# The first MLP of a four-layer transformer block kernel: second layer by token, contexts loaded earlier, norm and modulation on another engine

## The chip, the cores and the metric

The kernel runs on one core of a Trainium2 chip. Five engines work side by side, each through its own instructions in the order in which they were issued, and wait for each other by semaphores: TensorE (PE in the profile, with its weight loads as PEld), VectorE (DVE), ScalarE (ACT), GpSimd (POOL) and SyncE (SP), whose queue issues the DMA transfers of this kernel. The metric is the device time of one execution in microseconds (us). Before the change it is 1635.87 us, the median of three runs (1634.98 to 1640.96).

## The reference

The input `x` has 128 batches of 64 tokens with 128 features; `cond` has one vector of 128 for each batch, `ctx` 64 tokens for each batch. Four layers follow one another, all in float32. What the change touches is the last third of the first layer:

```python
mod = silu(t_emb) @ adaln_w + adaln_b
sh_sa, sc_sa, g_sa, sh_ff, sc_ff, g_ff = split(mod[:, None, :], 6)
...
xm = _ln(x) * (1.0 + sc_ff) + sh_ff
h = gelu(xm @ fc1_w + fc1_b, approximate=True)
x_ff = h @ fc2_w + fc2_b
x = x + g_ff * x_ff
```

`_ln` is a layer norm without weights, `fc1_w` is 128 x 512, `fc2_w` 512 x 128. Ahead of this the layer has a self attention and a cross attention; layer 1 is a cross attention with modulated norms of its own, layer 2 has the form of layer 0 with normed contexts, layer 3 is a mixture of experts.

## The kernel before

The 8192 tokens lie in 16 groups of 512 (8 batches); a group is a tile `xs[s]` of 128 partitions x 4 x 128, where a partition is a token and the last axis the features. All 16 groups stay in SBUF for the whole kernel. The order of all instructions is written out by hand: each engine takes them as the Python code emits them.

The stages are: the attentions of layer 0 (self, then cross, 16 groups each, `steps_1`), the first MLP (`turns_0`), the three attentions of layers 1 and 2 (`steps_2`), the second MLP (`turns_2`), layer 3. The last seven attention steps overlap the start of the following MLP, and the last turns of an MLP hold the preparation of the next stage: `into_mlp` (L1199) puts five heads of the MLP between attention steps, then turns 0 to 3 beside the last four steps, which close the last groups (`finish`, L522, with its normalization L548, bias L550 and projection L554). From turn 11 on `ahead_2` prepares the first groups of layer 1 (`prepare`, L378).

One MLP turn j (L733) works on several groups at once: the norm of group j+2, the hidden layer of group j in four parts, the output layer of group j-1 in four parts between them, the entry (transposition and modulation) of group j+1, the statistics of group j+3. In the first MLP the steps are as follows.

- `measure` (L662): layer norm statistics by VectorE (L312, L314), 1/std by GpSimd (L321, and a power, L322).
- `norm` (L665): GpSimd negates the mean (L361) and norms the four quarters (L364).
- `enter` (L668): four transposes on TensorE (L334, `psT`), then `modulated` (L337): VectorE multiplies (L339), GpSimd adds (L340), and the result `xm` has the features in the partitions.
- `hidden` (L671): a matmul of 128 x 512 (L675) and a gelu on ScalarE (L676).
- `output` (L678): the result `py` has features in the partitions; four parts accumulate (L681).
- `gate` (L704): VectorE adds the bias and multiplies by the gate (L706).
- `leave` (L711), one turn later: four transposes turn the result back to tokens (L714, `psB`), VectorE adds it to `xs` (L715) and takes the statistics that layer 1 will need (`x_mv`).
- `measure_context` (L646), in `beside_0` (L1180): SP loads the context of group j (L649), VectorE takes its statistics, GpSimd makes two reciprocal deviations and two products (L653, L321, L322, L656). They are used by layers 1 and 2. Beside it the tables for later layers are made (`later_tables`, L284), one piece in each of the first turns.

The second MLP has the forms `output_by_token` (L686, four matmuls of 128 x 128 for each quarter of the tokens, L691), `bias_by_token` (L696, L697 on GpSimd) and `leave_by_token` (L699; L701 and L702 on VectorE), which need no transposition: tokens are in the partitions of `py` at once. The gate and the gate times the bias then must lie in token layout; they come from a small table in DRAM (`gate_table`, L214), from which `gate_tile` (L273) loads 256 KB for each group by two broadcasting DMAs (L278).

`modulated_by_batch` (L343) is used by the attentions: ScalarE does the multiplication and the addition at once, one instruction for each of the 8 batches of a group (L351). SBUF tiles of one tag take turns in two buffers as a rule ("cm" for the contexts, "gt" for the gates), and so do the PSUM tiles "mm" (psT, psB, tables); "ph" has four buffers, "py" two.

Of the kernel before, what the change touches and what calls it, by code (L numbers as in the profile page):

```python
# [9 lines left out]
F32 = mybir.dt.float32  # L10
AF = mybir.ActivationFunctionType
ALU = mybir.AluOpType
# [3 lines left out]
P = 128  # L16
NST = 16
TT = 4
NB = 8
L = 64  # L20
NT = TT * P
# [38 lines left out]
def tile_kernel(ctx: ExitStack, tc: tile.TileContext, a: dict, out: bass.AP):  # L60
    nc = tc.nc
    V, S, G, T = nc.vector, nc.scalar, nc.gpsimd, nc.tensor
# [3 lines left out]
    def const(shape, name):  # L66
        return cp.tile(shape, F32, tag=name, name=name)

    x_d = a["x"].rearrange("b n c -> (b n) c").rearrange("(s t p) c -> s p t c", t=TT, p=P)
    ctx_d = a["ctx_1024"].rearrange("b n c -> (b n) c").rearrange("(s t p) c -> s p t c", t=TT, p=P)  # L70
# [11 lines left out]
    w = {}  # L82
# [11 lines left out]
    xs = [const([P, TT, P], f"x{s}") for s in range(NST)]  # L94
# [12 lines left out]
    for name, n in (("L0_xcond_ca_proj_b", P), ("L1_xcond_bp", P), ("L2_xcond_b_cproj", P), ("L3_xcond_router_b", 3)):  # L107
        t = const([P, n], name)
# [10 lines left out]
    ident = const([P, P], "ident")  # L119
# [7 lines left out]
    class Places:  # L127
# [9 lines left out]
    pools = [  # L137
        Places(),
        stack.enter_context(tc.tile_pool(name="mm", bufs=2, space=PSUM)),
        None,  # L140
        None,
        None,
    ]
# [38 lines left out]
    def col(name, i=0):  # L182
        r = _ROW[name] + i
        return vec[:, r : r + 1]
# [83 lines left out]
    def in_two(f, *of):  # L268

        kept = []  # L270
        return lambda: kept.append(f(*of)), lambda: kept[0]()
# [23 lines left out]
    def mod(name, i, s):  # L295

        return mods[name][:, i, ts(s, NB)].unsqueeze(2).broadcast_to([P, NB, L])

    def by_batch(t):
        return t.rearrange("p (b l) -> p b l", b=NB)  # L300
# [6 lines left out]
    x_mv = const([P, NST, TT, 2], "x_mv")  # L307

    def stats(pool, src, mv):
        st = pool.tile([P, TT, 6], F32, tag="st", name="st")  # L310
        for t in range(TT):
            V.bn_stats(st[:, t, :], src[:, t, :])  # L312
        for t in range(TT):
            V.bn_aggr(mv[:, t, :], st[:, t, :])  # L314
# [15 lines left out]
    def transposed(psum, src):  # L330

        ps = psum.tile([P, 512], F32, tag="mm", name="psT")
        for t in range(TT):
            T.transpose(ps[:, ts(t, P)], src[:, t, :], ident)  # L334
        return ps

    def modulated(pool, ps, name, scale, shift, s, tag="xm"):  # L337
        xm = pool.tile([P, NT], F32, tag=tag, name=tag)
        V.tensor_tensor(by_batch(xm), by_batch(ps), mod(name, scale, s), ALU.mult)  # L339
        G.tensor_tensor(by_batch(xm), by_batch(xm), mod(name, shift, s), ALU.add)  # L340
        return xm
# [17 lines left out]
    def normed_by_pool(pool, src, mv, rs, tag, engine=G):  # L359
        nmu = pool.tile([P, TT], F32, tag="nmu" + tag, name="nmu")  # L360
        G.tensor_scalar(nmu, mv[:, :, 0], -1.0, 0.0, ALU.mult, ALU.add)  # L361
        xn = pool.tile([P, TT, P], F32, tag=tag, name=tag)
        for t in range(TT):
            engine.tensor_scalar(  # L364
                xn[:, t, :], src[:, t, :], nmu[:, t : t + 1], rs[:, t : t + 1], ALU.add, ALU.mult
            )
        return xn
# [275 lines left out]

    def measure_context(s):  # L646
        pool = pools[0]
        c = pool.tile([P, TT, P], F32, tag="cm", name="c")
        nc.sync.dma_start(c, ctx_d[s])  # L649
        mv = pool.tile([P, TT, 2], F32, tag="mvc", name="mvc")  # L650
        stats(pool, c, mv)
        nmu = pool.tile([P, TT], F32, tag="nmuc", name="nmuc")
        G.tensor_scalar(nmu, mv[:, :, 0], -1.0, 0.0, ALU.mult, ALU.add)  # L653
        for eps in ctx_rs:
            rs = power(ctx_rs[eps][:, s], mv, eps)
            G.tensor_tensor(ctx_nb[eps][:, s], nmu, rs, ALU.mult)  # L656

    def mlp(wmod, w1, b1, w2, b2, beside, mv_out=None, by_token=False):

        pool, psum = pools[:2]  # L660

        def measure(d):  # L662
            d["mv"], d["rs"] = stats_of(pool, xs[d["s"]], 1e-6)

        def norm(d):  # L665
            d["xn"] = normed_by_pool(pool, xs[d["s"]], d["mv"], d["rs"], "xn")

        def enter(d):  # L668
            d["xm"] = modulated(pool, transposed(psum, d["xn"]), wmod, 4, 3, d["s"])

        def hidden(d, f):  # L671
            if f == 0:
                d["h"] = pool.tile([P, 4, NT], F32, tag="e", name="h")
            ph = pools[2].tile([P, 512], F32, tag="ph", name="ph")
            T.matmul(ph, w[w1][:, 0, ts(f, P)], d["xm"], start=True, stop=True)  # L675
            S.activation(d["h"][:, f, :], ph, AF.Gelu_apprx_tanh, bias=col(b1, f))  # L676

        def output(d, f):  # L678
            if f == 0:
                d["py"] = pools[3].tile([P, 512], F32, tag="py", name="py")  # L680
            T.matmul(d["py"], w[w2][:, f, :], d["h"][:, f, :], start=f == 0, stop=f == 3)  # L681

        def gates_of(d):
            d["gt"] = gate_tile(pool, d["s"], w2)

        def output_by_token(d, t):  # L686

            if t == 0:
                d["py"] = pools[3].tile([P, TT, P], F32, tag="py", name="py")
            for f in range(4):  # L690
                T.matmul(  # L691
                    d["py"][:, t, :], d["h"][:, f, ts(t, P)], w[w2][:, f, :],
                    start=f == 0, stop=f == 3,
                )

        def bias_by_token(d):  # L696
            G.tensor_tensor(xs[d["s"]], xs[d["s"]], d["gt"][:, :, 1, :], ALU.add)  # L697

        def leave_by_token(d):  # L699
            y = pool.tile([P, TT, P], F32, tag="y", name="y")  # L700
            V.tensor_tensor(y, d["py"], d["gt"][:, :, 0, :], ALU.mult)  # L701
            V.tensor_add(xs[d["s"]], xs[d["s"]], y)  # L702

        def gate(d):  # L704
            d["y"] = pool.tile([P, NT], F32, tag="y", name="y")
            V.scalar_tensor_tensor(  # L706
                by_batch(d["y"]), by_batch(d["py"]), col(b2), mod(wmod, 5, d["s"]),
                ALU.add, ALU.mult,
            )

        def leave(d):  # L711
            pt = psum.tile([P, 512], F32, tag="mm", name="psB")
            for t in range(TT):
                T.transpose(pt[:, ts(t, P)], d["y"][:, ts(t, P)], ident)  # L714
            V.tensor_add(xs[d["s"]], xs[d["s"]], pt.rearrange("p (t c) -> p t c", t=TT))  # L715
            if mv_out is not None:
                stats(pool, xs[d["s"]], mv_out[:, d["s"]])

        ds = [dict(s=s) for s in range(NST)]

        def go(f, j, *more):
            if 0 <= j < NST:
                f(ds[j], *more)

        heads = [
            lambda: go(measure, 0),
            lambda: go(norm, 0),
            lambda: go(measure, 1),
            lambda: (go(enter, 0), go(norm, 1)),
            lambda: go(measure, 2),  # L730
        ]

        def turn(j):  # L733
            out = output_by_token if by_token else output
            go(norm, j + 2)
            go(hidden, j, 0)
            go(out, j - 1, 0)
            go(hidden, j, 1)
            go(out, j - 1, 1)
            go(enter, j + 1)  # L740
            go(measure, j + 3)
            if by_token:
                go(bias_by_token, j - 1)
            go(hidden, j, 2)
            go(out, j - 1, 2)
            if 0 <= j < NST:
                beside(j)
            go(hidden, j, 3)
            go(out, j - 1, 3)
            if by_token:  # L750
                go(leave_by_token, j - 1)
                go(gates_of, j)
            else:
                go(gate, j - 1)
                go(leave, j - 2)

        return heads, [lambda j=j: turn(j) for j in range(NST + 2)]


# [412 lines left out]
    def stages():  # L1172
        ats = [attention_of(s, layer) for layer in ("L0s", "L0c") for s in groups]
        ats[0]["first"] = True
        ahead_1, steps_1 = attend(pools, ats)
# [3 lines left out]

        def beside_0(j):  # L1180
            measure_context(j)
            if j < len(later_tables):
                later_tables[j]()

        def beside_2(j):
            for f in l3_parts.get(j - 4, ()):
                f()

        heads_0, turns_0 = mlp(
            "L0_xcond_adaln_w", "L0_xcond_fc1_w", "L0_xcond_fc1_b", "L0_xcond_fc2_w",  # L1190
            "L0_xcond_fc2_b", beside_0, mv_out=x_mv,
        )
        heads_2, turns_2 = mlp(
            "L2_xcond_W_mod", "L2_xcond_W_mlp1", "L2_xcond_b_mlp1", "L2_xcond_W_mlp2",
            "L2_xcond_b_mlp2", beside_2, by_token=True,
        )
        last = 5

# [32 lines left out]
            f()  # L1231
        first_mods[2]()
        n = last + 2 + len(heads_0)
        for f in steps_1[6:-n]:
            f()
        rest = into_mlp(steps_1, heads_0, turns_0)
        second = [(0, 1, 2), (0,), (1, 0), (0, 0, 1, 2), (0, 1, 1, 2, 0, 0, 3, 3)]
        n_ = len(second)
# [66 lines left out]
```

## Time and profile before

| | |
|---|---|
| median of the runs | 1635.87 us |
| the profiled execution | 1636.9 us |
| its span, first to last instruction | 1635.1 us |
| mean granted TensorE clock | 0.994 |
| busy: PE, DVE, ACT, POOL | 97%, 79%, 64%, 66% |
| first hidden matmul of the first MLP to first scores of layer 1 | 412.51 to 552.91 us |

Of the views used below, the stretches give the busy time of each engine between two moments. A timeline row gives the start, the duration, the engine, the line, the operation with the tiles written and read, and how many instructions were merged; a bracket is idle time of the engine ahead of it and what ended it. Names drop their digits: `L_xcond_fc_w` is `fc1_w` or `fc2_w` of layer 0, `L_xcond_W_mlp` those of layer 2. A matmul of float32 takes two instructions, and their ends are modelled, so the distance from one start to the next is the better measure of TensorE.

### The profile page before, as it was taken

The page shows a single profiled execution, that of the slowest core. Times are in us where ns is not written, and L with a number is a line of the kernel's source. Part 1 is how long each engine was busy: PE and PEld are TensorE (multiplying, and loading weights), DVE is VectorE, ACT ScalarE, POOL GpSimd, SP SyncE. Part 2 cuts the span into 40 slices and gives each one's busy share as a digit, 9 for nine tenths or more (in the row PEclk, how much of TensorE's full clock was granted, in tenths as well). Part 3 has the DMA queues.
Part 4 walks back from the last instruction along what each step waited for, and adds up shares of the span by engine and source line. Part 5 has one row for each costly group of instructions (what it writes and reads, how often), then busy time and mean ns, then how long its engine had stood idle before and what let it go on. Part 6 is the DMA issues. An engine that isn't in the chain of part 4 may idle for free.

```text
span 1635.1 us, 64936 instructions
## 1 busy us (share of the span) xinstructions
PE 1581.5 (97%) x27842; PEld 1090.9 (67%) x27842; DVE 1296.4 (79%) x2430; ACT 1038.6 (64%) x1714; POOL 1079.4 (66%) x1814
## 2 busy tenths in 40 slices
PE   6999999998999899999999999998999999999998
PEld 4677767776554467777777677776777666666665
DVE  6999989999566688899999999998454566666666
ACT  5778767776333587788887888886334544444443
POOL 5688777775899888986787786665876333333322
PEclk9999999999999999999999999999999999999999
DMA  7333443322202012211333432221432111111100
GB/s 208 82 93 85 109 118 87 93 81 60 62 27 58 27 47 72 63 47 47 95 86 92 102 99 62 72 56 53 125 91 77 31 37 40 39 34 33 36 11 20
DMA packets 146783, 112.71 MB, mean 69 GB/s; under 512 B 36357, under 2 KB 125247, under 8 KB 146495
## 3 DMA queue, kind: packets, MB, share of 16 engines
q1 hardware_dynamic: 146288, 108.53, 25.0%
q8 instruction: 219, 3.59, 0.9%
q14 instruction: 69, 0.57, 0.1%
q10 hardware_dynamic: 207, 0.03, 0.0%
HBM read 83.99 MB, written 14.02 MB: 60 GB/s over the span
## 4 chain that ended last, share of the span: by engine, by line
PE 79%; DVE 13%; ACT 3%; POOL 2%; issue 1%; DMA 1%; SPq 1%; POOLq 0%; DVEq 0%
PE sc L470 9%; PE pp L495 9%; PE po L512 7%; PE ph L1062 6%; PE ph L675 6%; PE ph L1063 6%; DVE mx L477 5%; DVE e L479 5%; PE po L1093 5%; PE psT L334 5%; PE pk L428 5%; PE py L554 4%; PE py L691 3%; PE pvv L451 3%; PE pq L441 3%; PE py L681 2%
## 5 line engine op out<-in xcount | busy, mean ns | idle before, releaser
L499 ACT ACTIVATE eT<-pp 128x1024 f32<-128x1024 f32 x320 | 329.8, 1030 | 162.5 <-PE pp L495 162.5
L477 DVE TENSOR_REDUCE mx<-sc 128x32 f32<-128x2048 f32 x160 | 366.6, 2291 | 61.8 <-PE sc L470 61.8
L479 DVE TENSOR_TENSOR e<-sc,mx 128x2048 f32<-128x2048 f32 x160 | 366.6, 2291 | 5.4
L495 PEld LDWEIGHTS pp<-ident,e 64*128 64x128 f32 x5120 | 185.1, 139 | 142.6 <-ACT eT L499 46.7
L436 POOL TENSOR_SCALAR kbd<-kT,mask 128x512 f32<-128x512 f32 x316 | 212.4, 689 | 44.0 <-ACT kT L430 41.2
L495 PE MATMUL pp<-ident,e 64*128 64x64 f32 x5120 | 228.9, 229 | 8.4 <-DVE e L479 4.7
L364 POOL TENSOR_SCALAR xn<-x,nmu,rs 128x128 f32<-128x128 f32 x508 | 223.0, 452 | 13.3
L548 POOL TENSOR_TENSOR oT<-o,rb 128x512 f32<-128x512 f32 x80 | 102.0, 1275 | 153.1 <-DMA rb<-recs 65.8
L470 PE MATMUL sc<-kbd,qT 32*64 32x256 f32 x5120 | 181.7, 391 | 16.2 <-DVE e L479 15.3
L676 ACT ACTIVATE h<-ph,vec 128x512 f32<-128x512 f32 x128 | 87.4, 688 | 153.1 <-PE ph L675 152.9
L512 PE MATMUL po<-eT,vbd 128*32 128x64 f32 x10240 | 178.6, 222 | 1.2 <-issue 1.2
L1069 ACT ACTIVATE h<-h 128x512 f32<-128x512 f32 x112 | 70.5, 630 | 148.0 <-DVE h L1065 129.1
L512 PEld LDWEIGHTS po<-eT,vbd 128*32 128x32 f32 x10240 | 152.1, 110 | 14.0 <-issue 1.7
L322 POOL TENSOR_TENSOR rs<-rs,nhalf 128x4 f32<-128x4 f32 x128 | 130.3, 1018 | 10.6
L470 PEld LDWEIGHTS sc<-kbd,qT 32*64 32x64 f32 x5120 | 98.3, 132 | 53.5 <-DVE e L479 19.3
L1065 DVE TENSOR_TENSOR h<-ph,ab 128x512 f32<-128x512 f32 x112 | 77.0, 688 | 55.7 <-PE ph L1063 55.5
L312 DVE BATCH_NORM_STATS2 st<-x 128x6 f32<-128x128 f32 x512 | 110.5, 278 | 0.6
L1098 DVE SCALAR_TENSOR_TENSOR acc<-po,pr,acc 128x128 f32<-128x128 f32 x192 | 67.3, 350 | 44.1 <-PE po L1093 39.5
L1062 PE MATMUL ph<-nx,w 128*128 128x512 f32 x192 | 99.9, 602 | 0.0
L520 ACT COPY o<-po 128x512 f32<-128x512 f32 x160 | 95.7, 598 | 5.7 <-PE po L512 3.5
L1063 PE MATMUL ph<-u,w_ev 128*128 128x512 f32 x192 | 98.0, 592 | 0.0
L1093 PEld LDWEIGHTS po<-w_2o,h 128*128 128x128 f32 x768 | 92.1, 192 | 8.7 <-issue 8.4
(261 smaller groups left out, 2851.8 us busy)
## 6 DMA issues: line engine op xcount, KB each, us to landing
rb<-recs SPq DMA_DIRECT2D x80, 256.0 KB
c<-in_ctx_dram SPq DMA_DIRECT2D x64, 256.0 KB
o<-o SPq DMA_DIRECT2D x320, 32.0 KB
gt<-gate_L_xcond_sa_proj_w SPq DMA_DIRECT2D x32, 256.0 KB
gt<-gate_L_xcond_W_proj SPq DMA_DIRECT2D x32, 256.0 KB
gt<-gate_L_xcond_W_mlp SPq DMA_DIRECT2D x32, 256.0 KB
x<-in_x_dram SPq DMA_DIRECT2D x16, 256.0 KB
ctxT<-cm SPq DMA_DIRECT2D x16, 256.0 KB
```

Source lines behind the costliest of these rows:

```text
L322: G.tensor_tensor(rs, rs, nhalf, ALU.pow)
L364: engine.tensor_scalar(xn[:, t, :], src[:, t, :], nmu[:, t : t + 1], rs[:, t : t + 1], ALU.add, ALU.mult)
L436: (V if at.get("first") else G).tensor_scalar(kbd[:, j], by_batch(kT), mask[:, j : j + 1], 1.0, ALU.mult, ALU.mult)
L470: T.matmul(sc[ts(h, L), g, ts(t2, 256)], qT[ts(g, 32), ts(b, L)], kbd[ts(g, 32), :, b, :], start=True, stop=True,)
L477: V.tensor_reduce(mx, sc.rearrange("p g (m k) -> p (g m) k", k=L), AX.X, ALU.max)
L479: V.tensor_tensor(e, sc.rearrange("p g (m k) -> p (g m) k", k=L), mx.unsqueeze(2).broadcast_to([P, 32, L]), ALU.subtract,)
L495: T.transpose(pp[:, h, ts(4 * g2 + 2 * i + t2, L)], e6[ts(h, L), 2 * gg + g2, t2, i], ident[ts(h, L), ts(h, L)],)
L499: S.activation(eT[:, gg], pp, AF.Exp, scale=HD ** -0.5)
L512: T.matmul(po[ts(g, 32), i, ts(2 * t2 + h, L)], at["vbd"][:, 4 * u + 2 * t2 + h, 2 * g + i, :], e7[:, g // 2, h, g % 2, i, t2, :], start=T ...
L1062: T.matmul(ps, wn, d["nx"], start=True, stop=False)
L1063: T.matmul(ps, we, d["u"], start=False, stop=True)
L1093: T.matmul(po[:, ex, :], d[q][:, ts(t, P)], k3["w_2o"][:, q, :], start=r == 0, stop=r == 1)
```

## The change

The first MLP takes the form of the second one: the output by token, the bias on GpSimd from a gate tile, the update of `xs` by VectorE from `py` and the gate tile, one turn earlier than before; the statistics `x_mv` follow there. The forms with `psB` are gone. The gate table for it is made in steps 7 and 9 of the first attention. From group 4 on (`by_act=4`) the norm of the first MLP is done by ScalarE, with a product of mean and 1/std made by GpSimd (`nb`), and the modulation by `modulated_by_batch`; groups 0 to 3 and the second MLP keep their forms. The loads of contexts are taken out of `measure_context`: the first two are issued after heads 3 and 4, and that of group j+2 in turn j, after the statistics of group j.

```diff
+    measured = {}
+
+    def load_context(s):
+        if s < NST:
+            measured[s] = pools[0].tile([P, TT, P], F32, tag="cm", name="c")
+            nc.sync.dma_start(measured[s], ctx_d[s])
+
     def measure_context(s):
-        pool = pools[0]
-        c = pool.tile([P, TT, P], F32, tag="cm", name="c")
-        nc.sync.dma_start(c, ctx_d[s])
+        pool, c = pools[0], measured[s]
         mv = pool.tile([P, TT, 2], F32, tag="mvc", name="mvc")
...
         def norm(d):
-            d["xn"] = normed_by_pool(pool, xs[d["s"]], d["mv"], d["rs"], "xn")
+            if d["s"] < by_act:
+                d["xn"] = normed_by_pool(pool, xs[d["s"]], d["mv"], d["rs"], "xn")
+                return
+            nb = pool.tile([P, TT], F32, tag="nmuxn", name="nb")
+            G.tensor_scalar(nb, d["mv"][:, :, 0], -1.0, 0.0, ALU.mult, ALU.add)
+            G.tensor_tensor(nb, nb, d["rs"], ALU.mult)
+            d["xn"] = pool.tile([P, TT, P], F32, tag="xn", name="xn")
+            for t in range(TT):
+                S.activation(
+                    d["xn"][:, t, :], xs[d["s"]][:, t, :], AF.Identity,
+                    bias=nb[:, t : t + 1], scale=d["rs"][:, t : t + 1],
+                )
 
         def enter(d):
-            d["xm"] = modulated(pool, transposed(psum, d["xn"]), wmod, 4, 3, d["s"])
+            f = modulated if d["s"] < by_act else modulated_by_batch
+            d["xm"] = f(pool, transposed(psum, d["xn"]), wmod, 4, 3, d["s"])
...
-        def leave_by_token(d):
+        def leave(d):
             y = pool.tile([P, TT, P], F32, tag="y", name="y")
             V.tensor_tensor(y, d["py"], d["gt"][:, :, 0, :], ALU.mult)
             V.tensor_add(xs[d["s"]], xs[d["s"]], y)
...
             if mv_out is not None:
                 stats(pool, xs[d["s"]], mv_out[:, d["s"]])
...
         def turn(j):
-            out = output_by_token if by_token else output
             go(norm, j + 2)
             go(hidden, j, 0)
-            go(out, j - 1, 0)
+            go(output, j - 1, 0)
             go(hidden, j, 1)
-            go(out, j - 1, 1)
+            go(output, j - 1, 1)
             go(enter, j + 1)
             go(measure, j + 3)
-            if by_token:
-                go(bias_by_token, j - 1)
+            go(bias, j - 1)
             go(hidden, j, 2)
-            go(out, j - 1, 2)
+            go(output, j - 1, 2)
             if 0 <= j < NST:
                 beside(j)
             go(hidden, j, 3)
-            go(out, j - 1, 3)
-            if by_token:
-                go(leave_by_token, j - 1)
-                go(gates_of, j)
-            else:
-                go(gate, j - 1)
-                go(leave, j - 2)
+            go(output, j - 1, 3)
+            go(leave, j - 1)
+            go(gates_of, j)
...
         def beside_0(j):
             measure_context(j)
+            load_context(j + 2)
...
-        for f in steps_1[6:-n]:
-            f()
+        table = in_two(
+            gate_table, "L0_xcond_adaln_w", "L0_xcond_fc2_w", 5, col("L0_xcond_fc2_b")
+        )
+        for k, f in enumerate(steps_1[6:-n]):
+            f((), [table[k // 2]] if k in (1, 3) else ())
+        for s in range(2):
+            heads_0[3 + s] = lambda s=s, f=heads_0[3 + s]: (f(), load_context(s))
```

In the new code `output`, `bias` and `leave` are the former `output_by_token`, `bias_by_token` and `leave_by_token`.

More of the change, by code (lines that the diff above doesn't have):

```diff
@@ L656, in measure_context, with mlp @@
             G.tensor_tensor(ctx_nb[eps][:, s], nmu, rs, ALU.mult)
-    def mlp(wmod, w1, b1, w2, b2, beside, mv_out=None, by_token=False):
+    def mlp(wmod, w1, b1, w2, beside, mv_out=None, by_act=NST):
         pool, psum = pools[:2]
@@ L676, in hidden, with output @@
             S.activation(d["h"][:, f, :], ph, AF.Gelu_apprx_tanh, bias=col(b1, f))
[L678 to L681, printed above, removed]
         def gates_of(d):
             d["gt"] = gate_tile(pool, d["s"], w2)
-        def output_by_token(d, t):
+        def output(d, t):
             if t == 0:
@@ L694, in output_by_token, with bias @@
                 )
-        def bias_by_token(d):
+        def bias(d):
             G.tensor_tensor(xs[d["s"]], xs[d["s"]], d["gt"][:, :, 1, :], ALU.add)
-        def leave_by_token(d):
+        def leave(d):
             y = pool.tile([P, TT, P], F32, tag="y", name="y")
@@ L702, in leave_by_token @@
             V.tensor_add(xs[d["s"]], xs[d["s"]], y)
[L704 to L715, printed above, removed]
             if mv_out is not None:
@@ L1190, in stages @@
             "L0_xcond_adaln_w", "L0_xcond_fc1_w", "L0_xcond_fc1_b", "L0_xcond_fc2_w",
-            "L0_xcond_fc2_b", beside_0, mv_out=x_mv,
+            beside_0, mv_out=x_mv, by_act=4,
         )
@@ L1194, in stages @@
             "L2_xcond_W_mod", "L2_xcond_W_mlp1", "L2_xcond_b_mlp1", "L2_xcond_W_mlp2",
-            "L2_xcond_b_mlp2", beside_2, by_token=True,
+            beside_2,
         )
```

## The prediction

> **What bounds the kernel now.** I read the page's busy rows first (TensorE 97% of the span), then the busy time in stretches, then the timeline of the first MLP engine by engine. Stretches of that MLP's middle (columns: stretch, length, then busy us and instructions of PE, weight load, DVE, ACT, POOL, then the TensorE clock, DMA share and GB/s):
>
> ```profile
> 440.00:470.00 30.00, 29.31 (x104) 15.38 (x103) 20.85 (x106) 9.63 (x14) 27.47 (x56) 1.00 0.09 27
> 470.00:500.00 30.00, 30.00 (x98) 15.10 (x97) 20.78 (x104) 10.31 (x15) 27.17 (x59) 1.00 0.14 40
> ```
>
> TensorE is full, GpSimd nearly (its gaps are 0.07 us between small instructions), ScalarE works a third of the time. The stage runs from 412.51 (first hidden matmul) to 552.91 (first scores of the next layer): 140.4 us, 8.6% of the span. The rest of the program keeps its order, but for one table in the first attention, so the stage is all that can move much. One turn of GpSimd, from norm to norm (start, duration):
>
> ```profile
> 466.77 0.19 POOL L361 TENSOR_SCALAR nmu<-mv 128x4 f32<-128x4 f32 x1
> 467.07 1.75 POOL L364 TENSOR_SCALAR xn<-x,nmu,rs 128x128 f32<-128x128 f32 x4
> 468.78 1.04 POOL L340 TENSOR_TENSOR xm<-xm,mod_L_xcond_adaln_w 128x512 f32<-128x512 f32 x1
> 469.91 0.20 POOL L321 TENSOR_SCALAR rs<-mv 128x4 f32<-128x4 f32 x1
> 470.19 1.02 POOL L322 TENSOR_TENSOR rs<-rs,nhalf 128x4 f32<-128x4 f32 x1
> 471.20 0.19 POOL L653 TENSOR_SCALAR nmuc<-mvc 128x4 f32<-128x4 f32 x1
> ...
> 474.45 0.20 POOL L656 TENSOR_TENSOR ctx_nb<-nmuc,ctx_rs 128x4 f32<-128x4 f32 x1
> 474.61 0.19 POOL L361 TENSOR_SCALAR nmu<-mv 128x4 f32<-128x4 f32 x1
> ```
>
> 474.61 - 466.77 = 7.84 us. TensorE in the same place:
>
> ```profile
> 465.85 0.60 PE L334 MATMUL psT<-ident,xn 128*128 128x128 f32 x4
> 466.29 1.02 PE L675 MATMUL ph<-xm,L_xcond_fc_w 128*128 128x512 f32 x2
> 467.15 1.02 PE L681 MATMUL py<-h,L_xcond_fc_w 128*128 128x512 f32 x2
> ...
> 469.95 0.60 PE L714 MATMUL psB<-ident,y 128*128 128x128 f32 x4
> 470.38 1.02 PE L675 MATMUL ph<-xm,L_xcond_fc_w 128*128 128x512 f32 x2
> ```
>
> From start to start a hidden or output part takes 0.86 and a set of four transposes 0.44, so a turn is 8 x 0.86 + 2 x 0.44 = 7.76, and 7.97 to 8.2 with a table. Two engines tie. Waits on POOL show where groups of the attention still end beside the MLP (1.2 us before the matmul at 428.14, 0.9 at 446.38), and at 526.27 (0.6).
>
> **The change, part by part.**
> - *psB goes* (16 x 0.44 = 7.0 on PE; DVE's 0.75 + 0.68 becomes 0.69 + 0.69). Output by token in the second MLP advances 0.89 per part where this one takes 0.86 (there a turn without extras goes from transpose at 1157.23 to 1164.67: 7.44 = 4 x (0.86 + 0.89) + 0.44). 64 x 0.03 = 1.9 come back. PE alone: -5.1 over the stage.
> - *GpSimd* from group 4 loses nmu, xn and xm (0.30 + 1.71 + 1.13, start to start = 3.14), gains the bias (L697, 1.27 there) and two tiny ones for nb (like L361 and L656: about 0.49). 7.84 - 3.14 + 1.25 + 0.49 = 6.44: no longer the bound. Groups 0 to 3 keep their norm and gain the bias.
> - *ScalarE* gains four norms per turn (nearest row L405: 1.67 for four, the next begins after 1.54) and eight modulations (L351: 2.48 for eight, next after 2.32). With four gelus (0.58 apart) 6.2 of 7.44: it fits, but in the engine's order norm stands *ahead of* gelu 0 and 1, and modulation ahead of gelu 2 and 3.
> - *Table loads.* The Trainium skill, "ScalarE: Activation LUTs", section "Table sets: the hidden batching unit", says to batch calls by set; a switch is put at some 2.66 us. By that rule alone gelu, identity, gelu, identity, gelu would be four switches a turn, over 100 us in all. The trace decides: here gelu follows eight identities, and no load stands between:
>
> ```profile
> 535.27 2.48 ACT L351 ACTIVATE cm<-psT,mod_L_xcond_Wss_kv 128x64 f32<-128x64 f32 x8 [1.56 <-PE psT L334]
> 537.60 0.72 ACT L676 ACTIVATE h<-ph,vec 128x512 f32<-128x512 f32 x1
> ```
>
> I take nothing.
> - *Contexts ahead*: DVE's four waits for c (6.8 us) go; only the first on GpSimd's path counts: 0.8. On SP a load for j+2 waits for DVE's statistics of c(j), with the gate load queued behind it. Those end about 4.8 into the turn; two issues (1.31 in the second MLP) are out at 6.6; rb took 3.4 from issue to use at 403.46, so the gates land near 10.5, and the bias needs them at 7.4 + 5.2 = 12.6. Hidden, with 2 us to spare; without it each us late is a us of bias.
> - *Gate table in attention*: DVE 0.34 + 0.41, PE 0.22, in a stretch where DVE and scores alternate without slack (11.92 us per group, DVE 94% busy). Between 0 and 1.0; I take +0.7, as DVE is the loop. SP's context loads among the finish DMAs wait for pvv of a group just done: 0.
>
> **The new loop.** I follow one round from the end of output 3 in turn j-1, which takes the start of turn j as zero. DVE: y starts 0.2 later, x update at 0.8, its statistics 1.5, those of group j+3 2.6, results on GpSimd at 3.9. GpSimd: rs 1.28, bias 1.23, context statistics 3.41, nb 0.49, to 10.3. nb belongs to norm(j+3) of the *next* turn, and gelu 0 of that turn is behind it. ScalarE: norm 1.54, two gelus 1.16, modulation 2.32, two gelus 1.3: 16.6. Output 0 of turn j+2 needs that last gelu; from there to output 3: 4 x 0.89 + 3 x 0.86 + 0.44 = 6.6, sum 23.2. That is three turns, 7.73 each, above PE's 7.44; with tables and the odd wait about 7.9. Before, turns 5 to 13 took (526.27 - 454.83)/9 = 7.94. So the stall hardly leaves: it moves from GpSimd's bound to a round trip through all engines.
>
> **The early turns** are worse. Starts of hidden 0, before and by my sum. Turn 2: 428.14, 427.3 (context early). From there GpSimd does rs, bias(0), context(1), nb(4): 433.9; norm(4) then lets gelu 0..3 of turn 2 through at 435.4 to 437.9, and output 0 of turn 3 waits for them. GpSimd goes on with xm, rs, bias(1), context(2), the two closing steps of group 31 (L548, L550: 2.54) and nb(5): 444.0. Norm(5), two gelus, modulation(4): xm at 449.3. Turn 4: 446.38 before, 449.3 now. Turn 5: 454.83, 457.5; turn 14: 526.27, about 529. In the tail the next layer's preparation fills GpSimd as before (kbd at 548.93, mine 549.0) and psB is absent: first scores at 552.91, now 553.6, and their first maximum 1 us later, since DVE does the last group's statistics ahead of it instead of behind.
>
> The sum: stage +1.7 to the first maximum, table +0.7, and 0.6 for a shared port (below): **+3**. On the profiled execution's span 1635.1 that is 1638.1, with its 1.8 around it 1639.9. The median of the runs is 1635.87, 1.0 under that execution's 1636.9: **1638.9**. A measurement tells about 0.5% (8.2 us) from no change, so this counts as the same.
>
> **Rivals.**
> - *TensorE gets its gain* (17%): if norm is never late (GpSimd ahead), -5.1, stalls of 3.3 ahead of the tail, 1.2 in it, +0.7: -8.9, 1627. For it: GpSimd at 6.44 falls below PE. Against: the order norm, gelu. Half of this case lies below 1627.7.
> - *The update contends* (25%), the slower side. Now DVE adds y from SBUF to x in SBUF, while before one operand was in PSUM. The Trainium skill, "SBUF — State Buffer", section "SBUF: two separate sides", says that a DVE operation with two SBUF inputs and a GpSimd operation that reads SBUF lock each other out for a whole instruction. The second MLP's rows (duration min/median/max in ns; then the timeline at the longest) show it once strongly:
>
> ```profile
> L702 DVE TENSOR_TENSOR x<-x,y x16: 691/693/1744, 1154.1 to 1276.7; 128x512 f32<-128x512 f32 x16
> ```
> ```profile
> 1162.28 1.27 POOL L548 TENSOR_TENSOR oT<-o,rb 128x512 f32<-128x512 f32 x1
> 1162.35 1.74 DVE L702 TENSOR_TENSOR x<-x,y 128x512 f32<-128x512 f32 x1 [0.29 <-POOL x L697]
> 1163.51 1.72 POOL L550 TENSOR_TENSOR x<-x,L_xcond_b_cproj 128x512 f32<-128x512 f32 x1
> ```
>
> By the row's median it costs nothing, by its mean 0.08 per update, by the rule up to 1.05. In the loop a us is a third of a us per turn; I take 0.2 x 0.33 x 10 = 0.6. At 1.05 on DVE and 0.35 on GpSimd each time: 1.4/3 x 10 = 4.7, and some 2 in the early turns: +9.5, 1645.4. It decides from about 0.9 us lost per turn.
> - *Table loads after all* (2%): 1.28 x 4 x 12 = 61 us, 1698. The rows above exclude it.
> - The remaining 56% is the forecast, 1632 to 1644.
>
> The range: the forecast's own, the better half of the second case down to 1630 and the contention up to 1648. Faster 9% (half of 17), slower 22% (most of 25 and 2), same 69%.
>
> **What will show it.** In the changed profile: ScalarE's norm waits on GpSimd's nb, and gelus start right behind it in bunches; PE waits for gelu at output 0 rather than for xm from POOL; transposes of group j are 7.7 to 7.9 apart; a stall of about 3 us near turn 4; x updates of 0.7 to 1.7 us. I am wrong if GpSimd stands idle ahead of nb (then 7.44 per turn and rival one), if updates are mostly above 1.2 us, or if SP's gate loads end the waits of the bias.

## The result, and the profile after

| | before | changed |
|---|---|---|
| median of 6 runs each | 1637.82 us | 1650.72 us |
| lowest to highest | 1634.98 to 1640.96 | 1646.94 to 1654.22 |
| span of the profiled execution | 1635.1 us | 1652.2 us |
| mean TensorE clock | 0.994 | 0.990 |

The change makes the kernel slower: the ratio is 1.008, with an interval of 1.0063 to 1.0096, some 13 us. The forecast was 1638.9, and the time lies outside its range of 1630 to 1648.

Whole spans hold other differences between executions: the first transposes of the first MLP, ahead of which only a small table differs, start between 411.1 and 418.5 us in the profiles below. So the stage is measured by its own length, from the transposes of group 1 (`psT` of its second `enter`) to the first maximum of layer 1 (L477, `mx`). It is cut at the transposes of groups 5, 6 and 14:

| us | group 1 to 5 | 5 to 6 | 6 to 14 | 14 to first maximum | stage |
|---|---|---|---|---|---|
| before | 35.58 | 8.20 | 62.84 | 34.08 | 140.70 |
| changed | 41.77 | 7.89 | 63.90 | 40.10 | 153.66 |
| difference | +6.2 | -0.3 | +1.1 | +6.0 | +13.0 |

The stage's 13.0 us fit the 12.9 by which the medians differ. The rest of the span was 4.2 longer too in this one execution of the changed kernel (1498.5 against 1494.4), but over all the profiles of this document it lies between 1491.7 and 1498.8 and doesn't follow the edits. Nearly all of the stage's loss sits at its two ends. The stretches of the changed kernel (stretch, length, busy us of PE, weight load, DVE, ACT, POOL, TensorE clock, DMA share, GB/s):

```profile
440.00:470.00 30.00, 25.93 (x143) 19.16 (x142) 14.63 (x82) 19.39 (x48) 21.04 (x41) 0.89 0.30 83
470.00:500.00 30.00, 29.26 (x176) 21.86 (x176) 18.57 (x107) 22.79 (x59) 23.71 (x46) 1.00 0.34 91
```

GpSimd fell from 27 busy us in 30 to 21 and 24, as the sum of the prediction said, and ScalarE doubled. But TensorE is no longer full, and in the first stretch its clock is 0.89. The waits of the changed kernel from 408 to 575 us (engine and line, waited for; total, times, longest):

```profile
DVE y L714 <- PE py L704: 37.2, 14, 7.5
ACT xn L680 <- POOL nb L677: 31.0, 11, 8.2
...
DVE x L715 <- POOL x L710: 11.5, 5, 3.5
...
PE sc L470 <- DVE e L479: 8.2, 1, 8.2
PE ph L693 <- ACT xm L351: 7.9, 5, 4.1
...
PE pq L441 <- DVE xm L339: 3.2, 1, 3.2
```

ScalarE's norm waits 31 us for GpSimd's tiny product `nb`, 11 times. TensorE's waits are few: 4.1 at once for a modulation, 3.2 at `pq`, and 8.2 at the second scores, which stand behind the late first maximum and so behind the end of the stage. Here is the first of them in the timeline of the changed kernel, the entry of turn 4:

```profile
444.58 1.05 PE L704 MATMUL py<-L_xcond_fc_w,h 128*128 128x128 f32 x8
445.16 0.20 POOL L677 TENSOR_TENSOR nb<-nb,rs 128x4 f32<-128x4 f32 x1
445.40 1.65 ACT L680 ACTIVATE xn<-x,nb,rs 128x128 f32<-128x128 f32 x4 [6.44 <-POOL nb L677]
...
446.95 1.24 ACT L694 ACTIVATE h<-ph,vec 128x512 f32<-128x512 f32 x2
...
448.09 2.46 ACT L351 ACTIVATE xm<-psT,mod_L_xcond_adaln_w 128x64 f32<-128x64 f32 x8
...
450.60 2.07 PE L693 MATMUL ph<-xm,L_xcond_fc_w 128*128 128x512 f32 x2 [4.07 <-ACT xm L351]
...
452.47 1.91 PE L704 MATMUL py<-L_xcond_fc_w,h 128*128 128x128 f32 x8
```

The chain is the predicted one: `nb`, norm, two gelus, modulation, `xm`; only then hidden 0, the first of the turn's four hidden matmuls, can start. What was not predicted stands in the durations: the pair of matmuls takes 2.07 where it takes 1.02 elsewhere, and a group of eight 1.91 instead of 1.05. The stretches around it, of the changed kernel as well, say why in their clock column:

```profile
446.50:449.30 2.80, 0.03 (x1) 0.00 (x0) 1.25 (x4) 2.80 (x9) 2.65 (x5) 1.00 0.11 26
449.30:450.60 1.30, 0.00 (x0) 0.00 (x1) 1.30 (x9) 1.30 (x6) 1.07 (x4) 0.51 0.00 0
450.60:456.10 5.50, 5.50 (x14) 3.42 (x15) 1.96 (x16) 3.33 (x7) 5.03 (x10) 0.50 0.42 117
456.10:458.00 1.90, 1.90 (x14) 1.63 (x14) 0.00 (x0) 1.14 (x3) 1.63 (x4) 0.99 0.34 85
...
555.10:558.50 3.40, 3.13 (x23) 1.63 (x24) 0.22 (x1) 0.69 (x1) 3.17 (x7) 0.51 0.00 0
```

The clock falls during the wait, at 449.3, and stays at half until 456.1. TensorE does its first 5.5 us of work in that time, which at full clock would take half as long, 2.8 us less. The same happens at 555 us, behind the wait of 3.2, for 3.4 us. That is the other end of the stage, the start of layer 1, in the timeline of the changed kernel:

```profile
550.58 1.02 POOL L322 TENSOR_TENSOR rs<-rs,nhalf 128x4 f32<-128x4 f32 x1
...
551.57 1.26 POOL L710 TENSOR_TENSOR x<-x,gt 128x512 f32<-128x512 f32 x1
552.87 0.69 DVE L715 TENSOR_TENSOR x<-x,y 128x512 f32<-128x512 f32 x1 [2.25 <-POOL x L710]
...
554.66 0.66 DVE L339 TENSOR_TENSOR xm<-psT,mod_L_xcond_Wss_q 128x512 f32<-128x512 f32 x1
...
555.37 2.07 PE L441 MATMUL pq<-xm,L_xcond_Wq 128*128 128x512 f32 x2 [3.19 <-DVE xm L339]
...
562.59 1.76 POOL L403 TENSOR_SCALAR cn<-c,ctx_rs,ctx_nb 128x128 f32<-128x128 f32 x4
562.75 1.12 PE L470 MATMUL sc<-kbd,qT 32*64 32x256 f32 x32
562.85 0.69 DVE L714 TENSOR_TENSOR y<-py,gt 128x512 f32<-128x512 f32 x1 [7.53 <-PE py L704]
...
565.71 1.26 POOL L710 TENSOR_TENSOR x<-x,gt 128x512 f32<-128x512 f32 x1
567.00 0.69 DVE L715 TENSOR_TENSOR x<-x,y 128x512 f32<-128x512 f32 x1 [3.46 <-POOL x L710]
...
568.80 2.26 DVE L477 TENSOR_REDUCE mx<-sc 128x32 f32<-128x2048 f32 x1
```

The bias of the last two groups (L710) is issued to GpSimd behind the preparation of layer 1 (L364, L403, L321, L322). VectorE has `y` and then waits for `x` with that bias, 2.25 and 3.46 us. VectorE works in order, so what it has next waits too: the first time `xm` of layer 1 and behind it TensorE's `pq`; the second time the first maximum, though its scores began at 562.75. Before the change there was no bias on GpSimd in the first MLP, and the update waited for TensorE alone.

### The profile page after: what moved, and what is told of

It is laid out like the page before. It is cut to its first block, busy times and chain, and to the rows that moved or that the text cites. A ratio compares the mean times of both kernels' runs of the same rounds, so it can differ in the third digit from the quotient of the medians.

```text
span 1652.2 us, 65751 instructions
## 1 busy us (share of the span) xinstructions
PE 1581.1 (96%) x28164; PEld 1120.2 (68%) x28164; DVE 1288.9 (78%) x2420; ACT 1082.0 (65%) x1858; POOL 1077.5 (65%) x1782
## 4 chain that ended last, share of the span: by engine, by line
PE 67%; DVE 9%; POOL 5%; ACT 4%; issue 1%; DMA 1%; SPq 1%; POOLq 0%; DVEq 0%
PE pp L495 7%; PE sc L470 7%; PE ph L1056 6%; PE ph L1057 6%; PE po L512 6%; PE po L1087 5%; PE ph L693 5%; PE py L704 4%; PE psT L334 4%; DVE mx L477 4%; DVE e L479 3%; PE pk L428 3%; PE py L554 3%; PE pvv L451 3%; PE pq L441 3%
## 5 line engine op out<-in xcount | busy, mean ns | idle before, releaser
L477 DVE TENSOR_REDUCE mx<-sc 128x32 f32<-128x2048 f32 x160 | 366.5, 2290 | 62.8 <-PE sc L470 62.7
L364 POOL TENSOR_SCALAR xn<-x,nmu,rs 128x128 f32<-128x128 f32 x460 | 203.6, 456 | 12.0
L322 POOL TENSOR_TENSOR rs<-rs,nhalf 128x4 f32<-128x4 f32 x128 | 130.7, 1021 | 10.7
```

The costliest lines, as they stand in the source:

```text
L322: G.tensor_tensor(rs, rs, nhalf, ALU.pow)
L364: engine.tensor_scalar(xn[:, t, :], src[:, t, :], nmu[:, t : t + 1], rs[:, t : t + 1], ALU.add, ALU.mult)
L477: V.tensor_reduce(mx, sc.rearrange("p g (m k) -> p (g m) k", k=L), AX.X, ALU.max)
```

## The experiments

Times are medians, with the kernel before measured beside each on the same chip; ratios are to that. "Stage" is the length defined above.

| kernel | us | before | ratio, interval | 1 to 5 | 6 to 14 | 14 to max. | stage |
|---|---|---|---|---|---|---|---|
| changed | 1650.72 | 1637.82 | 1.008, 1.0063 to 1.0096 | 41.77 | 63.90 | 40.10 | 153.66 |
| e1 last biases on VectorE | 1645.29 | 1638.61 | 1.0046, 1.0029 to 1.0064 | 42.02 | 63.90 | 33.11 | 146.92 |
| e2 norm behind gelu | 1639.13 | 1638.61 | 1.0003, 0.9989 to 1.0016 | 33.30 | 60.43 | 39.84 | 141.48 |
| e3 both | 1629.51 | 1638.61 | 0.9951, 0.9932 to 0.9969 | 33.30 | 60.43 | 31.57 | 133.20 |
| e4 idle time filled | 1648.39 | 1638.61 | 1.0065, 1.0047 to 1.0083 | 39.08 | 63.89 | 40.09 | 150.95 |
| e5 all on GpSimd | 1665.75 | 1636.20 | 1.0188, 1.0172 to 1.0204 | 39.74 | 75.77 | 46.85 | 170.25 |
| e6 both, loads in turn | 1638.09 | 1636.20 | 1.0012, 1.0003 to 1.0020 | 36.85 | 60.43 | 35.74 | 141.10 |
| e7 table alone | 1638.08 | 1636.20 | 1.0004, 0.9995 to 1.0013 | 37.30 | 62.85 | 33.94 | 142.28 |
| e8 other biases on VectorE | 1651.43 | 1636.20 | 1.0092, 1.0078 to 1.0106 | 40.65 | 62.65 | 40.92 | 152.11 |
| e9 changed, loads in turn | 1658.52 | 1637.33 | 1.0138, 1.0124 to 1.0152 | 43.64 | 63.88 | 44.43 | 159.84 |
| e10 early loads alone | 1637.76 | 1637.33 | 1.0003, 0.9990 to 1.0016 | 34.81 | 62.85 | 34.10 | 139.95 |
| e11 ScalarE from group 2 on | 1631.79 | 1637.33 | 0.9965, 0.9951 to 0.9979 | 32.79 | 60.43 | 31.55 | 132.66 |

How well these lengths repeat can be read from kernels with the same code in a part. The middle is 62.84, 62.85 and 62.85 (before, e7, e10) and 63.88 to 63.90 (changed, e1, e4, e9), the tail 33.94 to 34.10 (before, e7, e10). The first part repeats less well: it has the same code in before and e7, and is 35.58 and 37.30. VectorE waited 1.03 us there for its first context in before and 2.73 in e7, and TensorE's longest wait was 1.18 and 2.88. So a single difference of 1 or 2 us in the first part says little.

**e1: the bias of groups 13 to 15 on VectorE**

```diff
         def bias(d):
-            G.tensor_tensor(xs[d["s"]], xs[d["s"]], d["gt"][:, :, 1, :], ALU.add)
+            E = V if mv_out is not None and d["s"] > 12 else G
+            E.tensor_tensor(xs[d["s"]], xs[d["s"]], d["gt"][:, :, 1, :], ALU.add)
```

> The changed kernel, but the gate bias of the last three groups (13 to 15) of the first MLP is added by VectorE instead of GpSimd, so that it no longer stands behind the next layer's preparation in GpSimd's queue. Queue theory: TensorE's wait for xm ahead of the q matmul (3.2 us) and VectorE's wait for the bias ahead of the first maximum (3.5 us) go; the first maximum of layer 1 comes 5 to 7 us earlier than in the changed kernel (568.8), so the kernel is 6 to 8 us slower than before instead of 13. Port theory (updates lose time to the shared port in every turn): three more additions with two SBUF inputs on VectorE, so no gain, 12 to 14 us slower. Loop theory (the round trip through all engines costs time in every turn): gain of 1 us at most.

The time is 6.7 us above before instead of 13. Only the last column moves: from 40.10 to 33.11, which is 1.0 below the 34.08 of before. The queue of GpSimd explains the tail, all of it.

**e8: the control.** The same three additions of work for VectorE and the same relief for GpSimd, but in the middle: groups 8, 9 and 10 (`d["s"] in (8, 9, 10)` in place of `d["s"] > 12`).

> The changed kernel with the gate bias of groups 8 to 10, instead of 13 to 15, added by VectorE: GpSimd is relieved of the same 3.8 us, in turns where nothing of the next layer stands ahead of the bias. If the gain of the earlier edit came from the place in GpSimd's queue, this one gives nothing: within 1.5 us of the changed kernel, 11 to 14 us slower than before. If it came from GpSimd's load, it gives the same: 6 to 8 us slower than before.

The tail stays at 40.92 and the time at 1.0092. So for the tail it isn't the load of GpSimd that matters, but what the late biases stand behind. (The middle, where these biases are, is 1.2 shorter, 62.65 against 63.90.)

**e2: ScalarE's norm is issued after the last gelu, not ahead of the first.** `nb` stays where it was on GpSimd.

```diff
             go(hidden, j, 3)
+            go(norm_by_act, j + 2)
             go(output, j - 1, 3)
```

(`norm_by_act` holds the four activations of `norm`.)

> The changed kernel, but ScalarE's four norm instructions of a turn are issued behind the turn's last gelu instead of ahead of its first one; GpSimd's part stays in its place. Queue theory: the stall ahead of turn 4 (4.1 us idle, then 6 us at half the TensorE clock) goes, transposes of group 5 come 5 to 6 us earlier than 456.9, and the turns shrink to about 7.5 us plus tables; 5 to 8 us slower than before instead of 13. Port theory: within 1 us of the changed kernel. Loop theory: the turns of groups 6 to 14 shrink (2 us in all), the stall ahead of turn 4 stays.

A miss in size: the gain against the changed kernel is 12 us, not 5 to 8. Both the early stall goes (41.77 to 33.30, below before's 35.58) and the loop is faster: 60.43 for 8 turns, 7.55 each, where the changed kernel takes 7.99 and TensorE alone would take 7.44. Two turns of ScalarE in the middle, first in the changed kernel, then in e2:

```profile
487.33 1.65 ACT L680 ACTIVATE xn<-x,nb,rs 128x128 f32<-128x128 f32 x4 [1.28 <-POOL nb L677]
488.88 1.24 ACT L694 ACTIVATE h<-ph,vec 128x512 f32<-128x512 f32 x2
490.02 2.46 ACT L351 ACTIVATE xm<-psT,mod_L_xcond_adaln_w 128x64 f32<-128x64 f32 x8
492.34 1.30 ACT L694 ACTIVATE h<-ph,vec 128x512 f32<-128x512 f32 x2
496.14 1.65 ACT L680 ACTIVATE xn<-x,nb,rs 128x128 f32<-128x128 f32 x4 [2.50 <-POOL nb L677]
```

```profile
487.61 2.48 ACT L351 ACTIVATE xm<-psT,mod_L_xcond_adaln_w 128x64 f32<-128x64 f32 x8 [0.64 <-PE psT L334]
489.94 1.30 ACT L700 ACTIVATE h<-ph,vec 128x512 f32<-128x512 f32 x2
491.08 1.68 ACT L686 ACTIVATE xn<-x,nb,rs 128x128 f32<-128x128 f32 x4
492.62 0.72 ACT L700 ACTIVATE h<-ph,vec 128x512 f32<-128x512 f32 x1
493.94 0.69 ACT L700 ACTIVATE h<-ph,vec 128x512 f32<-128x512 f32 x1 [0.60 <-PE ph L699]
```

In the changed kernel gelus stand behind a norm that waits, in pairs. In e2 the norm finds `nb` done and waits for nothing; gelu and modulation wait for TensorE, as they should where TensorE is the bound.

**e3: both edits**

> Both edits together. Queue theory: the gains add, 10 to 14 us under the changed kernel: within 2 us of the kernel before, on either side. Port theory: still over 10 us slower than before. Loop theory: 9 to 11 us slower than before.

Another miss, on the good side: 9.1 us below before by the medians, 0.5% by the ratio, and so faster than both kernels. The parts add, and somewhat more: the stage falls by 6.7 with e1, by 12.2 with e2, by 20.5 with both. The end of the stage in e3:

```profile
542.89 0.69 DVE L721 TENSOR_TENSOR y<-py,gt 128x512 f32<-128x512 f32 x1 [5.47 <-PE py L710]
543.62 0.81 DVE L722 TENSOR_TENSOR x<-x,y 128x512 f32<-128x512 f32 x1
...
545.53 2.26 DVE L477 TENSOR_REDUCE mx<-sc 128x32 f32<-128x2048 f32 x1
```

The update follows `y` at once, and the first maximum comes 2.6 us after `y` instead of 6.0.

**e4: the clock.** Four matmuls of 128 x 512 are added ahead of hidden 0 of turn 4, from the identity and `fc1_w` into a PSUM tile that nobody reads; they are extra work in the idle time.

```diff
             go(norm, j + 2)
+            if mv_out is not None and j == 4:
+                dm = pools[3].tile([P, 512], F32, tag="py", name="dm")
+                for _ in range(4):
+                    T.matmul(dm, ident, w["L0_xcond_fc1_w"][:, 0, :], start=True, stop=True)
```

> The changed kernel with four additional 128x512 matmuls of a constant into a PSUM tile that nobody reads, ahead of the first hidden matmul of turn 4, where TensorE stands idle for 4.1 us. If the half clock behind that wait is the price of standing idle, the following matmuls run at 0.86 from start to start at once, transposes of group 5 come 2 to 3 us earlier than 456.9, and the kernel is 2 to 3 us faster than the changed one. If the slow matmuls have another cause, nothing changes (within 1 us), or it is slower by the 3.4 us of the matmuls if TensorE isn't really idle there.

TensorE in e4 at the same place:

```profile
446.19 3.60 PE L738 MATMUL dm<-L_xcond_fc_w,ident 128*128 128x512 f32 x8
450.44 1.13 PE L693 MATMUL ph<-xm,L_xcond_fc_w 128*128 128x512 f32 x2 [0.65 <-ACT xm L351]
451.40 1.05 PE L704 MATMUL py<-L_xcond_fc_w,h 128*128 128x128 f32 x8
```

Hidden 0 comes no earlier than in the changed kernel (450.44; the stage began 0.2 earlier), but what follows runs at full pace, and the first part of the stage is 2.7 shorter. The medians differ by 2.3, which the intervals alone would not tell from nothing; the shift in the stage and the durations do.

Two other kernels have the same wait and another price. In e1 6.0 us of work fell into the half clock, in e8 3.4, in the changed kernel 5.5. Half of that is 3.0, 1.7 and 2.8; taken from their first parts of 42.02, 40.65 and 41.77 it leaves 39.0 each time, and e4, without half clock, has 39.08. So the half clock accounts for the loss behind the wait, and its size differs from trace to trace with the same wait of 4.1 us.

**e5: the norm and the addition of the modulation left to GpSimd for all groups** (`by_act=4` taken out of the call), the rest of the change kept.

> The changed kernel with the norm of all groups and the addition of the modulation left on GpSimd, so that ScalarE takes no part: what the output by token costs without the move to ScalarE. Queue theory: no gelu waits behind a norm, but GpSimd's turn is 7.84 + 1.25 = 9.1 us and sets the pace: 15 turns at 9.1 instead of 7.9, plus the tail's 7 us: 20 to 27 us slower than before. If the move to ScalarE was itself the loss, this kernel is faster than the changed one (under 13 us slower than before).

29.5 us above before, a little more than expected; the turns take 9.47 us. ScalarE's part of the change is thus needed: GpSimd can't take the bias on top of the norm.

**e7: the kernel before with the gate table alone** (the last hunk of the diff without the loads; the table is made and not used).

> The kernel before, with nothing changed but the gate table for the first MLP made in steps 7 and 9 of the first attention (nobody reads it). Prediction's term: 0.7 us slower than before, between 0 and 1.0. If it costs nothing, the stage starts at the same time (first transposes at 414.3 within what the runs differ).

0.0004, with zero inside the interval, which reaches from -0.8 to +2.1 us; the estimate of 0.7 us agrees with it and isn't proved by it.

**e6 and e9: the loads of contexts back in their own turn**, in e3 and in the changed kernel:

```diff
         def beside_0(j):
+            load_context(j)
             measure_context(j)
-            load_context(j + 2)
...
-        for s in range(2):
-            heads_0[3 + s] = lambda s=s, f=heads_0[3 + s]: (f(), load_context(s))
```

> The kernel with both edits (bias of the last groups on VectorE, ScalarE's norm behind the gelus), but each context is loaded in the turn that measures it, as before the change. VectorE then waits for the context in the early turns, where the last attention groups' transfers share SP's queue: 1 to 4 us slower than with both edits, so 5 to 8 us faster than before. If the early loads are hidden anyway, within 1 us of it (8 to 10 us faster than before).

> The changed kernel with each context loaded in its own turn, right ahead of its statistics, as before the change; the rest of the change stays. My prediction put the early loads at 0.8 us: by that this takes about 1651.5, 1 us more than the changed kernel. The rival, from the pair of kernels with both repairs (1629.5 and 1638.1): VectorE waits 2 to 4 us for c in the first turns, GpSimd's nmuc waits for the statistics, and nb stands behind nmuc in GpSimd's queue, so the lateness runs on into norm, gelu and output; then 6 to 10 us more than the changed kernel, 1657 to 1661.

e6 is a miss: not 1 to 4 but 8.6 us above e3 by the medians. e9, whose second expectation rests on that, came out so: 1658.5, some 8 above the changed kernel. In both, about 4 of the 6 to 8 us by which the stage grows sit in the tail. **e10** tries the same loads the other way, ahead of their turn in the kernel before, with no other part of the change:

> The kernel before with the early context loads alone. By my prediction's step 0.8 us faster than before (only the first wait stood on GpSimd's path), 1635.5 to 1637. If late contexts cost as much here as in the pair with both repairs, 5 to 9 us faster. I take the first, since before the change the order of GpSimd is full at 7.84 us a turn and takes up a wait of VectorE behind it; with a stage length from first transposes to the next layer's first maximum of 139 to 141 us.

There the time is the same, with an interval of the ratio from 0.9990 to 1.0016. The stage is 0.75 shorter, all of it in the first part, where so small a difference isn't shown to be one. So the early loads are not worth 6 to 8 us by themselves; beside the new gate loads they are. SP's queue waits in e9 (in total, times, longest) point to the reason:

```profile
SPq L278 <- DVE y L714: 54.7, 9, 11.4
```

The gate loads wait there for VectorE's `y`, that is for their buffer, and the next context load stands behind them on SP. Then VectorE waits for the context, GpSimd for VectorE's statistics, and `nb` stands behind that. The timeline of e9, in the early turns:

```profile
431.64 0.87 DVE L312 BATCH_NORM_STATS2 st<-c 128x6 f32<-128x128 f32 x4 [3.47 <-DMA c<-in_ctx_dram]
...
435.46 0.19 POOL L658 TENSOR_SCALAR nmuc<-mvc 128x4 f32<-128x4 f32 x1
...
439.52 0.20 POOL L677 TENSOR_TENSOR nb<-nb,rs 128x4 f32<-128x4 f32 x1
...
439.75 1.65 ACT L680 ACTIVATE xn<-x,nb,rs 128x128 f32<-128x128 f32 x4 [9.58 <-POOL nb L677]
```

The tail of e6 has the same chain: VectorE waits 4.38 us for a context at 517.23, GpSimd 2.9 for its statistics, and TensorE 2.04 for `cn`, which GpSimd makes, with half clock behind it.

With loads two turns ahead, SP's gate loads in the changed kernel wait for `y` only twice, 11.9 us in all. Its context loads now wait 59.1 us, 11 times, for VectorE's statistics, but so early that VectorE waits for no context any more. That the gate loads are the reason is read from the traces; no run here puts them on another queue.

**e11: ScalarE takes norm and modulation from group 2 on**, in e3 (`by_act=2`).

> The kernel with both repairs, and ScalarE taking norm and modulation from the third group on instead of the fifth. ScalarE still has the last attention groups' work in those turns, GpSimd their closing steps: if GpSimd is what is late in the early turns, 1 to 3 us faster than the 1629.5 of the kernel with both repairs, if ScalarE's queue is, 1 to 4 slower.

Neither: the stage is 0.5 shorter, in the first part, and the intervals of e3 and e11 overlap. Where ScalarE begins is open and matters little.

## Why the prediction was wrong

The stage was forecast at +1.7 and came out at +13.0. Point by point:

- **The loop was right.** The round trip through all engines was put at 23.2 for three turns plus extras, 7.9 a turn. The transposes of groups 5, 8, 11 and 14 are at 456.91, 480.91, 504.95 and 528.70: 24.0, 24.0 and 23.8 for three turns. From hidden 0 of turn 4 to turn 14 the sum had 0.2 less than before (+2.9 became +2.7), and from group 5 to 14 it became 0.8 more: 1.0 us in all. And e2 shows the named cause to be the cause: with norm out of the way of gelu the loop falls to 7.55.
- **The early stall was right in its place and chain, and too small by half.** The prediction had hidden 0 of turn 4 at 449.3; less the later start of the stage (0.8) it came at 449.8. Its +2.9 was +3.4 up to there. The step that failed is the one after it: from there on the sum let TensorE run at full pace, with no term for the clock. It ran at half clock for 5.5 us of work, which e4 prices at 2.7 us. Of the +6.2, 2.7 is clock.
- **The tail failed.** The sentence was: "In the tail the next layer's preparation fills GpSimd as before [...] first scores at 552.91, now 553.6, and their first maximum 1 us later". It followed GpSimd's work of layer 1 and VectorE's statistics, and did not put the biases of groups 14 and 15 into GpSimd's queue there, behind that work. By the sum the tail should have been 1.0 shorter than before; it was 6.0 longer. With those biases off GpSimd (e1) it is 1.0 shorter, and with other biases off it (e8) it stays long. So the whole 7.0 is that one term. It contains the half clock at 555 us, which e1 doesn't have.
- **Shared port: not the cause.** The updates of the changed kernel, over both MLPs (duration in ns, shortest, median, longest):

```profile
L715 DVE TENSOR_TENSOR x<-x,y x32: 691/693/1744, 430.8 to 1291.9; 128x512 f32<-128x512 f32 x32
```

  Shortest, median and longest are those of the second MLP before, and the longest is of the second MLP again: the 16 updates of the first take 0.69 to 0.73. Beside 8 of these 16 a small operation of GpSimd is longer instead, 0.50 to 0.74 in place of 0.20 (0.56 for L321 at 438.81, beside the update at 438.62), and the loop holds 24 us for three turns with that in it. The rival's 9.5 us (9.1 by its own terms: 1.7, 0.7, 4.7 and 2) were not there; its time of 1645.4 would have been nearer to the result, for a reason that the trace denies.
- **Table loads**: none between norm, gelu and modulation, as the rows of before said. The prediction set a rule of "Table sets: the hidden batching unit" against them (the 2.66 us stand in that page's "What ACT_TABLE_LOAD costs"), and read it too strictly: the same section says that cheap functions such as identity are in every set, so that rule and rows agree. The changed kernel has one load ahead of the stage's first gelu, 1.28 us at 414.48, and the next at 568.03 for the exponentials of layer 1, as the kernel before has.
- **Contexts and table**: 0.8 and 0.7 agree with what e10 and e7 measured on the kernel before (ratios of 1.0003 and 1.0004), and are too small for either to show. That the early loads guard the gate loads was seen only in part: the prediction had gates behind contexts on SP, not contexts behind gates.
- **Rival one**, TensorE getting its gain, was priced at 1627, and the point that spoke against it was "the order norm, gelu". With that order changed, and the bias moved, e3 takes 1629.5, 8 to 9 below before where the rival had 8.9: the arithmetic held.
- **Readings of before**: TensorE's wait ahead of 446.38 is 0.69 in the timeline, not 0.9, and hidden 0 of turn 5 starts at 454.67, not 454.83. Neither changes the argument.

Summed from the forecast's +1.7: 0.5 for the stall, 2.7 for the clock behind it, 1.0 in the middle, 7.0 in the tail give 12.9, against 13.0 measured.

## What to carry to other kernels

When a step moves to another engine, write out that engine's whole queue where the stage ends as well as in its middle: what stands ahead of the moved step there, and who waits behind its result. An operation with a late input should be issued behind those that are ready, however short it is: moving ScalarE's norm behind the gelus was worth 12 us, without changing any work. A stall of 3 to 4 us on TensorE is to be priced with the slow clock behind it: 1.7 to 3.0 us more in the changed kernel, e1 and e8.

## What the runs showed of the hardware

TensorE's clock falls during a wait of 4.07 us and stays at half for 6.8 us, of which 5.5 are work; e4 prices that at 2.7 us on top of the wait. In the changed kernel it falls at 408.4, 449.3, 555.1 and 568.8 us, which are 12, 31 and 4 times 3.41 us apart, and it stays low for 3.4, 6.8, 3.4 and 10.2. So these falls lie on a beat of their own, and two waits of one length can have different prices. The Trainium skill, "TensorE: Matmul & The Clock Gate", section "What's actually happening", puts the fall after at least one idle window of about 3.4 us and the release after a busy one, with windows that run freely. By that rule work that begins inside a window is slow for 3.4 to 6.8 us, an estimated loss of 1.7 to 3.4 us; the losses of 1.7, 2.8 and 3.0 us above lie in it. The fall doesn't agree: it came 2.8 us after TensorE's last work here, and after less in e6, where TensorE waited 2.04 us for `cn`. A wait of 2.88 in e7 left the clock as it was. The stretches of e6, of e8 with its late fall in the same wait of 4.07, and of e7:

```profile
531.60:533.70 2.10, 0.06 (x2) 0.02 (x1) 1.96 (x4) 0.20 (x1) 2.10 (x5) 1.00 0.00 0
533.70:537.10 3.40, 3.40 (x10) 2.10 (x11) 1.47 (x9) 1.61 (x6) 3.02 (x9) 0.51 0.91 219
537.10:540.00 2.90, 2.90 (x19) 2.18 (x18) 1.67 (x10) 2.01 (x5) 2.82 (x4) 0.99 0.07 20
...
449.30:453.30 4.00, 0.00 (x0) 0.00 (x0) 2.49 (x11) 4.00 (x13) 3.62 (x8) 1.00 0.08 17
453.30:456.70 3.40, 3.34 (x9) 2.31 (x10) 2.02 (x16) 2.87 (x8) 3.07 (x7) 0.51 0.09 15
...
427.40:430.30 2.90, 0.06 (x1) 0.00 (x0) 2.50 (x12) 0.00 (x0) 2.78 (x6) 1.00 0.00 0
430.30:434.00 3.70, 3.66 (x10) 1.70 (x11) 0.81 (x2) 1.37 (x2) 3.17 (x8) 1.00 0.14 26
```

So the length of a wait alone doesn't say whether it has this price. A possible reason: counted in steps of 3.41 us from its later fall at 561.9, a beat of e7 lies at 428.8, inside the wait, so that less than half of each step was idle, while the wait of e6 lies in one step. No run was made to test this, and what in a wait decides it stays open.
